# Quantised integers of two BitLinear layers: rounding constant taken off before the transposes, which then move bfloat16 halves

## The chip, the cores and the metric

The kernel runs on one core of a Trainium2 chip. The metric is device time in microseconds. Before the change the median of nine runs is 669.87 us (667.6 to 670.4).

Engines are named as in the profile: PE is TensorE (PEld its weight loads), DVE VectorE, ACT ScalarE, POOL GpSimd and SP SyncE, which issues most of the DMAs.

## The reference, cut to what matters

A small transformer of four layers runs over x of 4 x 256 tokens with 256 features, each layer with an attention and a feed-forward block, all with residuals. The change touches the feed-forward blocks of layers 1 and 2, whose matmuls quantise both operands:

```
def act_quant(x):
    scale = 127.0 / jnp.clip(jnp.max(jnp.abs(x), axis=-1, keepdims=True), EPS)
    return jnp.clip(jnp.round(x * scale), -128.0, 127.0) / scale
def weight_quant(w):
    scale = 1.0 / jnp.clip(jnp.mean(jnp.abs(w)), EPS)
    return jnp.clip(jnp.round(w * scale), -1.0, 1.0) / scale
h = jax.nn.silu(bitlinear(x, w1)) * bitlinear(x, w3)   # layer 1, 704 hidden
return bitlinear(h, w2)
```

Layer 2 does the same with 1024 hidden features and biases. So each row of activations becomes whole numbers from -127 to 127 times one scale per row, and each weight -1, 0 or 1 times one scale. Such numbers are exact in bfloat16.

## The kernel before, in words

The 1024 tokens are eight tiles of 128 rows (two per batch). Before the last feed-forward block, everything is emitted by `layers(nk)`. Its coroutines each describe one piece of work as a sequence of `Op`s: an engine, an assumed duration, the buffers read and written, and new buffers wanted (PSUM banks, and SBUF slots "a2", "a4", "sc"). `Flow.run` (L182) keeps a planned clock per engine. It takes next the operation whose planned start plus `PULL` times its coroutine's due time is smallest, emits the instructions, and moves on. The result is a fixed order on PE, DVE, ACT, POOL and SP. The due times stand in `DUE` by stage (L82, plus `SKEW` per batch) and in `DUE_WEIGHTS` (L83). `func` on an `Op` marks Silu and Exp, for which the trace has ACT load a function table at each switch (1283 ns); the planner charges 1.3 us. The emitted program holds this plan for two cases of the token ids (`nk` 1 and 2); the run takes `nk` = 1.

A tile goes through `token_tile` (L1305): `attention1`, then `ffn1(t)` (L1249). When both tiles of a batch are done, `batch(b)` (L1353) runs the attention of layer 2 and then `ffn2(t)` (L1386) for both, and starts `attention3` of the batch. Layer 3 ends per tile in `tile3`, which routes tokens: POOL scatters eight copies of each row to DRAM by indirect DMA (`hs`, L1677). After the last scatters the experts' stage begins (L1895), which is the same in both kernels.

Both feed-forward functions follow one scheme:

1. `norms` (L850): statistics on DVE, the power -1/2 on POOL (L861), normed rows on DVE (L864).
2. `scales` (L1208): the greatest magnitude of each row (DVE, L1211 to L1213), its products with the weights' means (POOL, L1217), then in place `src * s + ROUND` on DVE (L1221). ROUND is 1.5 * 2^23, so the sum rounds to a whole number, and the tile then holds that number plus ROUND in float32.
3. `turned_ints` (L1224): float32 transposes on PE in chunks of 128 columns, up to four into one PSUM bank (L1235); ACT copies them out to `qT` in bfloat16 and takes ROUND off through the bias (L1239; L1244 for the last chunk of 64 columns in layer 1).
4. Matmuls with the ternary weights, bfloat16 (L1270, L1407), Silu on ACT, the product on DVE (L1277) or POOL (L1422).
5. `scales` and `turned_ints` again over the hidden rows, 704 or 1024 wide, and the last matmul (L1288, L1430).

Of the kernel before, what the change touches and what calls it, by code (L numbers as in the profile page):

```python
# [22 lines left out]
BF16 = mybir.dt.bfloat16  # L23
I32 = mybir.dt.int32
AF = mybir.ActivationFunctionType
ALU = mybir.AluOpType
AX = mybir.AxisListType

P = 128
B, S, D = 4, 256, 256  # L30
# [7 lines left out]
ROUND = 1.5 * 2.0**23  # L38
# [27 lines left out]
def chunks_of(n):  # L66
    return [(i, min(P, n - i)) for i in range(0, n, P)]


PE, DVE, ACT, POOL, SP = "PE", "DVE", "ACT", "POOL", "SP"  # L70
# [8 lines left out]

LATER = 20.0  # L80
PULL, SKEW = 0.00368, 28.0
DUE = dict(x0=0.0, f0=50.0, x1=70.0, f1=100.0, x2=140.0, f2=190.0, q3=140.0, h3=260.0, t3=240.0)  # L82
DUE_WEIGHTS = dict(fp8=80.0, f1=170.0, p2=330.0, f2=160.0, win=250.0, kv=240.0, p3=200.0)  # L83


class Buf:
# [27 lines left out]
class Flow:  # L114
# [21 lines left out]
    def go(self, gen, due=0.0):  # L136
        th = Thread(gen, due)
        self.threads.append(th)
        self.resume(th, None)
        return th  # L140
# [10 lines left out]
    def release(self, *bufs):  # L151

        for b in bufs:
            self.roles[b.role][b.slot] = max(b.used, b.ready or 0.0)
# [76 lines left out]
def model(ctx: ExitStack, tc: tile.TileContext, a: dict, out: bass.AP):  # L231
    nc = tc.nc
# [11 lines left out]
    def scal(n, name):  # L244
        return small.tile([P, n], F32, tag=f"s{n}", name=name)

    def held(pool, shape, name, dtype=F32):
        return pool.tile(shape, dtype, tag=name, name=name)
# [7 lines left out]
    ident = held(const, [P, P], "ident")  # L256
    make_identity(nc, ident)
    identb = held(const, [P, P], "identb", BF16)
# [5 lines left out]
    rnd = held(const, [P, 2], "rnd")  # L264
# [150 lines left out]
    def layers(nk):  # L415
# [4 lines left out]
        def due(b, stage):  # L420
            return DUE[stage] + SKEW * b

# [18 lines left out]
        def bank(shape, name):  # L441
            return ("bank", shape, name)
# [7 lines left out]
        def sc(name):  # L450
            return ("sc", [P, 16], name)
# [165 lines left out]
        def fp8_weights():  # L617
            for o in range(0, 2 * I0, CH):
                for k in range(2):
                    yield from fp8_piece(loads[("w0_gate", "w0_up")[k]], FP8[k][o // CH], o, CH)  # L620
            for o in range(0, 6 * D, CH):
                yield from fp8_piece(loads["w0_down"], FP8[2][o // CH], o, CH)
# [585 lines left out]
        def scales(src, n, k_means):  # L1208

            s = yield Op(DVE, 0.36 + 0.00122 * n, (src,), new=[sc("am")])  # L1210
            nc.vector.tensor_reduce(s[:, 0:1], src.ap, AX.X, ALU.max, apply_absolute_value=True)  # L1211
            nc.vector.tensor_scalar(s[:, 0:1], s[:, 0:1], QEPS, 1.0 / 127.0, ALU.max, ALU.mult)
            nc.vector.reciprocal(s[:, 1:2], s[:, 0:1])  # L1213
            back = Buf()
            yield Op(POOL, 0.18 * len(k_means), (s, *[m for m, _ in k_means]), (back,))
            for k, (_, col) in enumerate(k_means):
                nc.gpsimd.tensor_tensor(  # L1217
                    s[:, 2 + k : 3 + k], s[:, 0:1], means[:, col : col + 1], ALU.mult
                )
            yield Op(DVE, 0.04 + 0.0008 * n, (s,), (src,))  # L1220
            nc.vector.tensor_scalar(src.ap, src.ap, s[:, 1:2], ROUND, ALU.mult, ALU.add)  # L1221
            return s, back

        def turned_ints(src, n, qT):  # L1224

            cs = chunks_of(n)
            groups = [cs[k : k + 4] for k in range(0, len(cs), 4)]
            tps = yield Op(
                PE, 0.122 * len(cs), (src,), new=[bank([P, len(g), P], "tp_q") for g in groups]
            )  # L1230
            if len(groups) == 1:
                tps = [tps]
            for g, tp in zip(groups, tps):
                for k, (o, w) in enumerate(g):
                    nc.tensor.transpose(tp.ap[:w, k, :], src.ap[:, o : o + w], ident)  # L1235
            for i, (g, tp) in enumerate(zip(groups, tps)):
                full = sum(w == P for _, w in g)
                yield Op(ACT, 0.13 + 0.00075 * full * P + (0.25 if full < len(g) else 0), (tp,), (qT,))
                nc.scalar.activation(  # L1239
                    qT[:, 4 * i : 4 * i + full, :], tp.ap[:, :full, :], AF.Identity, bias=rnd[:, 1:2]  # L1240
                )
                if full < len(g):
                    w = g[-1][1]
                    nc.scalar.activation(  # L1244
                        qT[:w, 4 * i + full, :], tp.ap[:w, full, :], AF.Identity, bias=rnd[:w, 1:2]
                    )
            release(*tps)

        def ffn1(t):  # L1249
# [4 lines left out]
            flat = Buf(h.ap[:, 0, :], h.role, h.slot, h.ready)  # L1254
            flat.used = h.used
            s, back = yield from scales(flat, D, [(Q1[0], 0), (Q1[1], 1)])
            yield from turned_ints(flat, D, qT)
            release(flat)
            n = I1 // 2
# [13 lines left out]
            for nh, (pg, pu, g) in enumerate(pre):  # L1273
# [6 lines left out]
                release(pg, pu, g)  # L1280
            release(s)
            s, back = yield from scales(hh, I1, [(Q1[2], 2)])
            yield from turned_ints(hh, I1, qT)
            release(hh)
            cs = chunks_of(I1)
# [100 lines left out]
        def ffn2(t):  # L1386
# [6 lines left out]
            flat = Buf(h.ap[:, 0, :], h.role, h.slot, h.ready)  # L1393
            flat.used = h.used
            s, back = yield from scales(flat, D, [(Q2[0], 3), (Q2[1], 4)])
            yield from turned_ints(flat, D, qT)
            release(flat)
            for nh in range(2):
# [298 lines left out]
        with tc.manual_schedule(engines=ORDERED | {mybir.EngineType.SP}):  # L1697
# [3 lines left out]
            for c in range(NCH):  # L1701
                go(chunk(c), due(2 * c, "x0"))
            w = DUE_WEIGHTS
            go(fp8_weights(), w["fp8"])
# [23 lines left out]
    def ps_tp(shape, name, dtype=F32):  # L1728
        return psum.tile(shape, dtype, tag="tp", name=name, bufs=2)
# [22 lines left out]
    def moe_tile(shape, tag, bufs):  # L1752
        return moe.tile(shape, F32, tag=tag, name=tag, bufs=bufs)
# [43 lines left out]
    with tc.If(rv > 0):  # L1797
        hTs = [moe_tile([P, 2, CH], "hT_left", 2) for _ in range(NCH)]
        for t in range(NT):
            h = layernorm(t, moe, 1)  # L1800
            tp = ps_tp([P, 2, P], "tp_h")
# [3 lines left out]
        with tc.For_i(0, E3, 1) as e:  # L1805
# [4 lines left out]
            for c in range(NCH):  # L1810
                pg, pu = ps_mm([I3, CH], "ps_g3"), ps_mm([I3, CH], "ps_u3")
                for k, ps in enumerate((pg, pu)):
                    for dc in range(2):
                        o = (2 * k + dc) * I3
# [3 lines left out]
                g = moe_tile([I3, CH], "g_left", 1)  # L1818
                nc.scalar.activation(g, pg, AF.Silu)
                nc.vector.tensor_mul(g, pu, g)  # L1820
                for k in range(TPC):
# [3 lines left out]
                    w = scal(1, "w_left")  # L1825
# [245 lines left out]
```

## Time and profile before

| | |
|---|---|
| median of 9 runs | 669.87 us |
| the profiled execution | 669.71 us |
| its span in the trace | 668.0 us |
| its mean granted clock | 0.973 |
| L1235 transposes | 144, from 116.9 to 363 us |
| start of the first and last scatter L1677 | 351.5 and 479.3 us |

Times in the profile count from the span's start. The page gives busy times of engines over the span. The chain of waits follows back from the last instruction, at each step to what released it. A group of instructions has its line, engine, operation, tiles and shapes, then count, busy time, mean duration in ns, and the engine's idle time just before them with what ended it. The last 188 us of the span are the experts' stage.

### The profile page before, as it was taken

To read this page: it belongs to the slowest core of one execution; us is meant where nothing else is said; L and a number is where in the kernel's file an instruction comes from. 1 tells how busy PE (TensorE), PEld (TensorE's weight loads), DVE (VectorE), ACT (ScalarE), POOL (GpSimd) and SP (SyncE) were. 2 spreads that over 40 slices of the span, in tenths; PEclk is the share of its full clock that TensorE was granted. 3 is DMA by queue.
4 is the path that set the end of the run, shared out by engine and by line. 5 is a ranking of instruction groups with operands and counts; after the bars stand their busy time and mean duration, and the time that the engine had idled before them with its cause. 6 is when DMAs were issued, how large, how long until landed. Compare 5 with 4: busy or idle time off the path is not lost.

```text
span 668.0 us, 11511 instructions
## 1 busy us (share of the span) xinstructions
PE 605.8 (91%) x3844; PEld 465.7 (70%) x3844; DVE 462.7 (69%) x1172; ACT 349.0 (52%) x898; POOL 403.3 (60%) x524
## 2 busy tenths in 40 slices
PE   5998699998999999999999899797299999999966
PEld 4764267676787777787778678674188788787754
DVE  5689857875969697599889788887434434434755
ACT  1244248869789874466866696566322222222210
POOL 6998995044454534647447868787746566566550
PEclk9999899999999999999999999899699999999997
DMA  8999999501200130000030111122499887777666
GB/s 292 372 386 235 220 226 239 146 25 29 83 2 1 64 111 2 0 1 1 2 95 33 57 56 47 57 88 85 141 290 357 263 278 252 236 237 215 218 201 233
DMA packets 57059, 98.15 MB, mean 147 GB/s; under 512 B 7121, under 2 KB 39624, under 8 KB 56992
## 3 DMA queue, kind: packets, MB, share of 16 engines
q1 hardware_dynamic: 47072, 78.40, 39.7%
q0 software_dynamic: 7680, 16.84, 7.3%
q10 hardware_dynamic: 2240, 2.10, 0.9%
q8 instruction: 32, 0.52, 0.3%
q14 instruction: 35, 0.29, 0.2%
HBM read 58.42 MB, written 43.07 MB: 152 GB/s over the span
## 4 chain that ended last, share of the span: by engine, by line
PE 53%; DVE 19%; ACT 9%; POOL 8%; issue 6%; DMA 4%; DVEq 0%; POOLq 0%; SPq 0%; ACTq 0%
PE ps_y L1930 7%; PE ps_g L1912 7%; PE ps_q L1463 5%; POOL hs L1677 3%; DVE act L1920 3%; PE ps_u L1912 3%; DMA hs<-hx,slots 2%; PE ps_p L700 2%; PE ps_y L1346 2%; PE ps_u L1078 2%; PE ps_s L1324 2%; PE ps_y L1567 2%; POOL q L1477 1%; PE tp_q L1235 1%; PE ps_p L896 1%
## 5 line engine op out<-in xcount | busy, mean ns | idle before, releaser
L1937 POOL DMA_INDIRECT yd<-yb,hb x84 | 82.5, 982 | 57.9 <-DVE yb L1935 38.6
L1677 POOL DMA_INDIRECT hs<-hx,slots x64 | 67.3, 1052 | 21.9 <-issue 11.3
L861 POOL TENSOR_TENSOR st<-st,mhalf 128x1 f32<-128x1 f32 x56 | 33.0, 593 | 60.5 <-DVE st L857 46.6
L1920 DVE TENSOR_TENSOR act<-ps_u,g 96x384 f32<-96x384 f32 x32 | 17.7, 554 | 65.1 <-ACT g L1918 35.9
L1510 ACT ACTIVATE e<-ps_s,nm 128x128 f32<-128x128 f32 x128 | 45.9, 404 | 15.7 <-DVE nm L1504 15.4
L1477 POOL TENSOR_TENSOR q<-rt 64x512 f32<-64x512 f32 x32 | 44.0, 1376 | 12.1 <-DVE rt L1473 7.4
L1930 PE MATMUL ps_y<-wt,act 96*64 96x256 f32 x336 | 42.4, 388 | 2.7 <-DVE act L1920 1.4
L1912 PE MATMUL ps_g<-hbT,wt 128*96 128x192 f32 x224 | 43.1, 336 | 0.0
L1912 PEld LDWEIGHTS ps_g<-hbT,wt 128*96 128x96 f32 x224 | 34.1, 162 | 10.8 <-issue 10.8
L1912 PE MATMUL ps_u<-hbT,wt 128*96 128x192 f32 x224 | 41.0, 326 | 0.0
L1935 DVE COPY yb<-ps_y 128x256 f32<-128x256 f32 x64 | 27.2, 425 | 19.7 <-PE ps_y L1930 19.5
L1935 ACT COPY yb<-ps_y 128x256 f32<-128x256 f32 x32 | 11.9, 373 | 47.0 <-DVE yb L1935 38.4
L1912 PEld LDWEIGHTS ps_u<-hbT,wt 128*96 128x96 f32 x224 | 36.4, 163 | 0.0
L1422 POOL TENSOR_TENSOR hh<-g,v 128x512 f32<-128x512 f32 x16 | 20.3, 1277 | 25.3 <-ACT g L1420 16.4
L1498 PEld LDWEIGHTS ps_s<-keys,q 128*128 128x128 f32 x256 | 34.5, 196 | 1.3
L1918 ACT ACTIVATE g<-ps_g 96x384 f32<-96x384 f32 x32 | 15.6, 487 | 36.5 <-PE ps_g L1912 36.5
L1498 PE MATMUL ps_s<-keys,q 128*128 128x128 f32 x256 | 34.6, 279 | 0.0
L1930 PEld LDWEIGHTS ps_y<-wt,act 96*64 96x64 f32 x336 | 21.6, 136 | 17.5 <-DVE act L1920 9.4
L1923 ACT COPY hbT<-tp_hb 128x384 f32<-128x384 f32 x31 | 14.8, 479 | 35.0 <-PE tp_hb L1839 35.0
L1239 ACT ACTIVATE qT<-tp_q,rnd 128x512 bf16<-128x512 f32 (+2 forms) x48 | 25.7, 567 | 12.4 <-PE tp_q L1235 12.3
L1510 ACT ACTIVATION_READ_ACCUMULATOR e<-ps_s,nm 128x1 f32 x128 | 30.6, 243 | 0.0
L864 DVE TENSOR_SCALAR h<-x,st 128x256 f32<-128x256 f32 x56 | 27.0, 494 | 5.0 <-POOL st L861 4.8
(345 smaller groups left out, 1728.1 us busy)
## 6 DMA issues: line engine op xcount, KB each, us to landing
hs<-blank_row SPq DMA_DIRECT2D x1, 12336.0 KB, 87.0
hb<-hs SPq DMA_DIRECT2D x28, 385.5 KB, 3.9
wt<-in_w_gu SPq DMA_DIRECT2D x14, 768.0 KB, 8.6
yd<-blank SPq DMA_DIRECT2D x1, 8192.0 KB, 28.9
wt<-yd SPq DMA_DIRECT2D x6, 1024.0 KB, 6.9
wt<-in_w_dn SPq DMA_DIRECT2D x14, 384.0 KB, 8.6
wo<-in_w_o SPq DMA_DIRECT2D x2, 1024.0 KB, 5.7
w<-in_w SPq DMA_DIRECT2D x2, 704.0 KB, 11.2
```

Of the source, the lines that this page charges most:

```text
L861: nc.gpsimd.tensor_tensor(s[:, 8:9], s[:, 7:8], mhalf, ALU.pow)
L864: nc.vector.tensor_scalar(h[:, k, :], x_t(t), ss[k][:, 6:7], ss[k][:, 8:9], ALU.subtract, ALU.mult)
L1463: nc.tensor.matmul(ps.ap[:, k, :], w[:, hp * P : (hp + 1) * P], qc.ap, start=True, stop=True)
L1477: nc.gpsimd.tensor_add(qv(q[i])[r, hps, :], t0[r], t1[r])
L1498: nc.tensor.matmul(s.ap[:, k, :], qv(q[hd % 2])[:, hd // 2, rows], keys3[:, hd % 2, b * S : b * S + nk * P], start=False, stop=k == n - 1,)
L1510: nc.scalar.activation(wide[:, k, :], s.ap[:, k, :], AF.Exp, bias=nm[:, k : k + 1], accum_out=tot[:, k : k + 1],)
L1677: put = nc.gpsimd.indirect_dma_start(out=hs[:, :], out_offset=bass.IndirectOffsetOnAxis(ap=slots[:, t, j : j + 1], axis=0), in_=rows[:, j, ...
L1912: nc.tensor.matmul(ps[:, i], gu[:, (e + i) % GROUP, 2 * k + dc, :], hbT[:, dc, :, i * (P // 2) : (i + 1) * (P // 2)], start=dc == 0, stop= ...
L1920: nc.vector.tensor_mul(act, pu, g)
L1930: nc.tensor.matmul(y[i * (P // 2) : (i + 1) * (P // 2), k], act[:, i, j, :], dn[:, (e + i) % GROUP, :], start=True, stop=True,)
L1935: (nc.scalar.copy if j == 1 else nc.vector.tensor_copy)(yb[:, j, :], y[:, k, :])
L1937: put = nc.gpsimd.indirect_dma_start(out=yd[:, :], out_offset=bass.IndirectOffsetOnAxis(ap=hbs[p][:, j, D : D + 1].bitcast(I32), axis=0), ...
```

## The change

`scales` takes ROUND off again itself. For the normed rows (256 wide, 16 calls) DVE subtracts it; for the hidden rows (704 or 1024 wide, 16 calls) POOL adds -ROUND, a column spread over the row. The tile then holds small whole numbers in float32, whose upper 16 bits are the same number in bfloat16. `turned_ints` transposes these upper halves, read with a stride of two, against the bfloat16 identity into bfloat16 PSUM tiles, and ACT copies them out without a bias. The planner is told half the duration for the transposes, and 10 of its 16 due times are others. Lines from L1250 on are 4 higher in the changed kernel; the transposes are L1243 and the evictions L1247 and L1250.

```diff
--- before.py
+++ after.py
@@ -79,8 +79,8 @@
 
 LATER = 20.0
 PULL, SKEW = 0.00368, 28.0
-DUE = dict(x0=0.0, f0=50.0, x1=70.0, f1=100.0, x2=140.0, f2=190.0, q3=140.0, h3=260.0, t3=240.0)
-DUE_WEIGHTS = dict(fp8=80.0, f1=170.0, p2=330.0, f2=160.0, win=250.0, kv=240.0, p3=200.0)
+DUE = dict(x0=10.0, f0=50.0, x1=70.0, f1=100.0, x2=135.0, f2=185.0, q3=150.0, h3=260.0, t3=220.0)
+DUE_WEIGHTS = dict(fp8=90.0, f1=170.0, p2=430.0, f2=170.0, win=260.0, kv=280.0, p3=200.0)
 
 
 class Buf:
@@ -1219,6 +1219,12 @@
                 )
             yield Op(DVE, 0.04 + 0.0008 * n, (s,), (src,))
             nc.vector.tensor_scalar(src.ap, src.ap, s[:, 1:2], ROUND, ALU.mult, ALU.add)
+            if n == D:
+                yield Op(DVE, 0.04 + 0.0008 * n, (src,), (src,))
+                nc.vector.tensor_scalar(src.ap, src.ap, ROUND, None, ALU.subtract)
+            else:
+                yield Op(POOL, 0.05 + 0.0024 * n, (src,), (src,))
+                nc.gpsimd.tensor_tensor(src.ap, src.ap, rnd[:, 1:2].to_broadcast([P, n]), ALU.add)
             return s, back
 
         def turned_ints(src, n, qT):
@@ -1226,24 +1232,22 @@
             cs = chunks_of(n)
             groups = [cs[k : k + 4] for k in range(0, len(cs), 4)]
             tps = yield Op(
-                PE, 0.122 * len(cs), (src,), new=[bank([P, len(g), P], "tp_q") for g in groups]
-            )
+                PE, 0.06 * len(cs), (src,), new=[("bank", [P, len(g), P], "tp_q", BF16) for g in groups]
+            )
+
+            ints = src.ap.bitcast(BF16).rearrange("p (i two) -> p i two", two=2)[:, :, 1]
             if len(groups) == 1:
                 tps = [tps]
             for g, tp in zip(groups, tps):
                 for k, (o, w) in enumerate(g):
-                    nc.tensor.transpose(tp.ap[:w, k, :], src.ap[:, o : o + w], ident)
+                    nc.tensor.transpose(tp.ap[:w, k, :], ints[:, o : o + w], identb)
             for i, (g, tp) in enumerate(zip(groups, tps)):
                 full = sum(w == P for _, w in g)
                 yield Op(ACT, 0.13 + 0.00075 * full * P + (0.25 if full < len(g) else 0), (tp,), (qT,))
-                nc.scalar.activation(
-                    qT[:, 4 * i : 4 * i + full, :], tp.ap[:, :full, :], AF.Identity, bias=rnd[:, 1:2]
-                )
+                nc.scalar.copy(qT[:, 4 * i : 4 * i + full, :], tp.ap[:, :full, :])
                 if full < len(g):
                     w = g[-1][1]
-                    nc.scalar.activation(
-                        qT[:w, 4 * i + full, :], tp.ap[:w, full, :], AF.Identity, bias=rnd[:w, 1:2]
-                    )
+                    nc.scalar.copy(qT[:w, 4 * i + full, :], tp.ap[:w, full, :])
             release(*tps)
 
         def ffn1(t):
```

## Prediction

> **What bounds the kernel now.** I read the page first (busy times, chain), then the busy times by stage, the chain piece by piece, PE's timeline, the groups by shape, and the answers for single lines.
>
> ```profile
> span 668.0 us, 11511 instructions
> ...
> PE 605.8 (91%) x3844; PEld 465.7 (70%) x3844; DVE 462.7 (69%) x1172; ACT 349.0 (52%) x898; POOL 403.3 (60%) x524
> ...
> PE 53%; DVE 19%; ACT 9%; POOL 8%; issue 6%; DMA 4%; DVEq 0%; POOLq 0%; SPq 0%; ACTq 0%
> ```
>
> TensorE is the busiest engine, and over half of the chain that ended last runs through it. By stage:
>
> ```profile
> 100.00:160.00 60.00, 57.72 (x493) 43.15 (x492) 44.70 (x121) 48.44 (x145) 19.75 (x31) 0.97 0.46 115
> 160.00:360.00 200.00, 196.43 (x1248) 155.12 (x1248) 162.81 (x404) 147.28 (x347) 107.15 (x138) 1.00 0.10 33
> 360.00:480.00 120.00, 97.15 (x590) 74.65 (x588) 96.02 (x279) 76.75 (x256) 93.55 (x149) 0.95 0.20 69
> ```
>
> Columns after the length: PE, PEld, DVE, ACT, POOL. The changed steps lie between 115 and 370 us, nearly all in the second row, where PE is busy 98% and DVE 81%, ACT 74%, POOL 54%. A busy matmul overlaps the next, so I also counted each matmul only until the next one's start, and no longer than its columns stream: about 181 of those 200 us. PE is the bound there, with some 19 us of true gaps. After 480 us come the experts; the change leaves them alone.
>
> **PE: 144 transposes, each half as long.** Eight tiles turn 2 + 6 chunks (ffn1) and 2 + 8 (ffn2): 8 × 18 = 144. What one costs on a full queue is read from the chain, whose pieces run from start to start:
>
> ```profile
> 243.33 0.66 PE tp_q L1235 x6
> 243.99 0.87 PE ps_y L1430 x8
> ...
> 272.92 0.43 PE ps_g L1407 x2
> ```
>
> A float32 transpose takes 0.66/6 = 0.110 us. The bfloat16 matmuls take 0.109 us for 256 columns (L1430) and 0.215 us for 512 (L1407): time follows columns. PE's timeline has one shorter kind, 64 columns with a full weight load before each:
>
> ```profile
> 456.38 0.34 PE L1599 MATMUL ps_pos<-sel,onesb 128*128 128x64 bf16 x6
> ```
>
> The last one alone lasts 0.19 us, so five steps take 0.15 us, 0.03 each. A 128-column bfloat16 transpose lies between, at 0.055 us: 144 × 0.055 = 7.9 us of PE's queue. Loads of strided halves exist already (the fp8 weights at L1078) and take 104 and 98 ns beside 98 for plain ones, so the stride is free. Of the 144, 76 stand on the chain, 9.2 us together; halved, 4.2 us leave the chain for certain. The rest also stand in the queue that is 90% full. I take −6.0 us, between 4.2 and 7.9; nothing at all is the end of a rival below.
>
> [...]
>
> **DVE: 16 more passes over the normed rows.** The constant is taken off by a second scalar operation of the same shape as L1221.
>
> ```profile
> L1221 DVE TENSOR_SCALAR h<-h,am 128x256 f32<-128x256 f32 x16 | 5.7, 361 | 0.1
> L1422 POOL TENSOR_TENSOR hh<-g,v 128x512 f32<-128x512 f32 x16 | 20.3, 1277 | 25.3 <-ACT g L1420 16.4 <-DVE w L1614 5.0 <-DVE v L1413 3.7
> L1239 ACT ACTIVATE qT<-tp_q,rnd 128x512 bf16<-128x512 f32 x24 | 15.8, 687 | 10.7 <-PE tp_q L1235 10.6
> L1275 ACT ACT_TABLE_LOAD x3 | 3.8, 1283 | 0.1
> ```
>
> 16 × 0.345 us (its undisturbed time) = 5.5 us. From 115 to 370 us DVE is busy 205.4 us, of which 36.0 lie on the chain, 17.5%: +1.0 us. DVE has 50 us of gaps there, so less is possible; all 5.5 is the other end.
>
> **POOL: 16 adds over the hidden rows.** The nearest row is L1422, two-input and of the same tiles: 1277 ns for 512 elements, 2.5 ns each. 704 elements give 1.76 us, 1024 give 2.55: 8 × 4.31 = 34.5 us. What hides it: POOL is busy 126.4 of the 255 us, so 129 are free. Each add is a new link: transposes that waited for DVE's L1221 now wait for POOL, and PE's whole queue stands behind them. On POOL the norms' powers (L861), the scale products (L1217) and the query sums (L1477) queue behind the add; DVE's L864 and with it the next tile's transposes wait for the powers. In the changed program's order all 16 adds stand ahead of the first scatter, so the scatters, POOL's load after 350 us, are not interleaved with them. L1422, same engine, same tiles, never appears on the chain in 16 times; I take 0. At POOL's mean share of the chain (26.0 of 126.4 us, 20.6%) it would be +7.1 us. If the cover goes, a tile's path is longer by 0.35 + 1.76 us in ffn1 and 0.35 + 2.55 in ffn2, 5.0 in all.
>
> A side effect on DVE: the same operation is slower beside POOL work.
>
> ```profile
> L864 DVE TENSOR_SCALAR h<-x,st x56: 395/408/1473, 10.4 to 395.3; 128x256 f32<-128x256 f32 x56
> L1527 DVE TENSOR_TENSOR e<-e,nm x32: 691/692/1905, 299.8 to 457.1; 128x512 f32<-128x512 f32 x32
> ```
>
> Beyond their medians these two lose 56 × (494 − 408) and 32 × (807 − 692) ns = 8.5 us in the whole run, beside about 215 us of POOL arithmetic. For 34.5 us more that is 1.4 us of DVE, at 17.5% +0.3 us.
>
> **ACT.** The 56 evictions become plain copies from bfloat16. No row has that input; the nearest copies (L1155, float32, same size) take 602 ns beside 687. From −0.085 × 24 = −2.0 us to +2.0; I take 0. The built program's order, instruction by instruction, holds something the diff does not tell: 19 function table loads before the experts instead of 15, since Silu and Exp are interleaved differently. 4 × 1.283 = 5.1 us of ACT; its share of the chain is 37.8 of 188.5 us, 20%: +1.0 us, from 0 to 5.1.
>
> **The order.** The due times move by up to 100 us (p2), and every engine's order changes with them. SP issues the same transfers in the same sequence; DMA costs stay. Summing row durations along PE's order, the last batch's first query product (L1463) stands behind 338 us of PE work, 345 before, so PE's saving is not spent in front of it. Whether the new order has more or fewer waits no row shows: PE's named waits from 100 to 380 us come to some 8 us, so −8 to +8; I take 0.
>
> **Sum.** The profiled execution took 669.7 us (span 668.0), practically the median, 669.9. −6.0 + 1.0 + 0 + 0.3 + 0 + 1.0 = −3.7: **666.0 us**.
>
> **Rivals.** *POOL takes PE's place* (slower). Place: the wait of the tp_q transposes, from 120 to 365 us. Price: chain terms alone: −4.2 + 1.0 + 0.3 + 1.0 + 7.1 = +5.2, 674.9 us. It decides once over half of the adds' 34.5 us × 20.6% shows; for it speaks that the adds double the POOL work of a hidden layer, against it POOL's 129 idle us and L1422. *The full PE gain* (better): 7.9 us, with 2.0 from the evictions, and DVE's, ACT's and contention's terms hidden: 659.8 us. For it: PE 90% full. *The transposes do not get cheaper*: the load of a float32 transpose takes 141 ns and a bfloat16 one 98, so if loads set the pace at 0.11 us, only the costs stay: 669.7 + 2.3 = 672.0 us. Against it: the 0.03 us row.
>
> **How the numbers follow.** Forecast 50%, POOL rival 25%, full gain 13%, no cheaper transposes 7%, 5% for an order that misses all of these. A measurement of this kernel can tell about 0.2% from no change, 1.3 us. Of the forecast's 50, 7 fall within that and 43 are faster; the full gain adds 13, the odd orders 2: 58% faster. Of the POOL rival's 25, 4 lie within, of the 7 one, making 12 with the forecast's; 30% are slower. The low end takes the full gain and 1.8 of the 8 us of waits, 658; the high end reaches the POOL rival, 675.
>
> **What would show it.** Right: tp_q start to start near 0.055 us; PE busy from 160 to 360 us without POOL as releaser of tp_q; the experts' first rows land some 4 us earlier. Wrong: waits "PE tp_q <- POOL hh" of several us, table loads on the chain beyond two, tp_q at 0.08 or more, or gaps on PE that come from the order and lie away from the changed lines.

## The result and the profile after

The changed kernel takes 675.50 us (median of 10 runs, 673.12 to 676.55); before, run beside it, takes 669.88 us (31 runs). The ratio is 1.0077, interval 1.0063 to 1.0091. I had forecast 666.0, between 658 and 675. The profiled execution took 676.24 us, its span 674.5.

The page of the changed kernel:

```profile
span 674.5 us, 11551 instructions
...
PE 607.6 (90%) x3844; PEld 460.8 (68%) x3844; DVE 477.6 (71%) x1188; ACT 349.5 (52%) x902; POOL 428.3 (63%) x540
...
PE 46%; DVE 26%; POOL 9%; issue 7%; ACT 6%; DMA 4%; POOLq 0%; DVEq 0%; SPq 0%; ACTq 0%
```

POOL and DVE got the work that was added, 25 and 15 us. The last line is the news: PE's share of the chain went from 53% to 46%, DVE's from 19% to 26%. By stage (columns after the length: PE, PEld, DVE, ACT, POOL):

```profile
100.00:160.00 60.00, 58.30 (x511) 43.03 (x509) 48.97 (x134) 51.15 (x154) 26.06 (x37) 1.00 0.50 130
160.00:360.00 200.00, 189.54 (x1203) 145.08 (x1204) 168.70 (x397) 139.43 (x322) 125.42 (x146) 0.97 0.08 27
360.00:480.00 120.00, 103.38 (x621) 79.81 (x619) 101.01 (x290) 82.18 (x278) 90.31 (x144) 0.94 0.19 66
```

In the second row PE is busy for 189.5 us where it had 196.4, but the stage is not shorter: the first scatter starts at 358.2 us, 351.5 before. The transposes themselves became as narrow as the change makes them. One piece of the changed kernel's chain (start, length, work), then its groups of new and changed operations by shape:

```profile
253.05 0.45 PE tp_q L1243 x8
```

```profile
L1227 POOL TENSOR_TENSOR hh<-hh,rnd 128x1024 f32<-128x1024 f32 x8 | 16.4, 2051 | 2.1 <-DVE hh L1221 1.8
L1227 POOL TENSOR_TENSOR hh<-hh,rnd 128x704 f32<-128x704 f32 x8 | 11.1, 1389 | 1.5 <-DVE hh L1221 1.2
L1224 DVE TENSOR_SCALAR h<-h 128x256 f32<-128x256 f32 x16 | 7.7, 490 | 0.2
L1247 ACT COPY qT<-tp_q 128x512 bf16<-128x512 bf16 x24 | 13.9, 595 | 1.5 <-PE tp_q L1243 1.4
```

A transpose takes 0.45/8 = 0.056 us from start to start, 0.110 before. The adds take 16.4 + 11.1 = 27.5 us of POOL, the evictions 595 ns where they took 687. But the subtraction's mean of 490 ns is far above its median of 294. DVE's and POOL's timelines show why, of the changed kernel, each line with start, length and what ran, and in brackets the idle time before it with what ended that:

```profile
319.38 0.30 DVE L1224 TENSOR_SCALAR h<-h 128x256 f32<-128x256 f32 x1
...
324.46 1.98 DVE L1224 TENSOR_SCALAR h<-h 128x256 f32<-128x256 f32 x1
```

```profile
320.96 3.04 POOL L1481 TENSOR_TENSOR q<-rt 64x512 f32<-64x512 f32 x2 [1.23 <-DVE rt L1477]
324.07 2.22 POOL L1227 TENSOR_TENSOR hh<-hh,rnd 128x1024 f32<-128x1024 f32 x1
```

The same subtraction takes 0.30 us without an add beside it and 1.98 us when it starts behind an add on POOL; it ends at 326.44, 0.15 us after the add. So I read it as DVE standing until the add is over, not as DVE running slower beside it. L864 and L1221 stand in the same way (L864 for 0.56 to 2.12 us where its median is 0.41; L1221 on the normed rows: 606 ns in the mean, 361 before). Eight of the 16 adds meet a DVE scalar operation over 256 columns (L864, L1221, L1224 or L1666). All eight of these end 0.149 to 0.152 us after their add, while they last 0.51 to 2.12 us, and together they last 8.4 us more than by their lines' medians. Reductions (L1211, 1.21 us over 1024 columns), statistics (L855, 0.42 us) and operations that read PSUM (L1417, 0.74 us) have the same lengths beside the adds as without. It works the other way too: an add over 1024 columns takes 1.89 us at its shortest, and 2.10 to 2.27 us in the four cases where L1221 or L1531 was already at work on DVE as it starts.

In one of the eight, L864 at 302.99 us, the DVE record begins 0.07 us ahead of the add's (303.06 us), and DVE stands all the same, for 2.12 us; that add keeps its 1.89 us. What makes DVE stand no run shows, only when it goes on.

Adding up, per form, what DVE's instructions from 115 to 372 us take beyond their lower quartile gives some 9 us in the before kernel and some 19 in the changed one.

### The profile page after: what moved, and what is told of

It reads as the page before. It is cut to its first block, busy times and chain, and to the rows that moved or that the text cites. A ratio compares the mean times of both kernels' runs of the same rounds, so it can differ in the third digit from the quotient of the medians.

```text
span 674.5 us, 11551 instructions
## 1 busy us (share of the span) xinstructions
PE 607.6 (90%) x3844; PEld 460.8 (68%) x3844; DVE 477.6 (71%) x1188; ACT 349.5 (52%) x902; POOL 428.3 (63%) x540
## 4 chain that ended last, share of the span: by engine, by line
PE 46%; DVE 26%; POOL 9%; issue 7%; ACT 6%; DMA 4%; POOLq 0%; DVEq 0%; SPq 0%; ACTq 0%
PE ps_y L1934 7%; PE ps_g L1916 7%; POOL hs L1681 3%; PE ps_g L1078 3%; DVE act L1924 3%; PE ps_u L1078 2%; PE ps_u L1916 2%; PE ps_y L1350 2%; PE ps_y L1127 2%; PE ps_q L1467 2%; DVE e L1531 2%; PE ps_s L1328 2%; DVE h L864 1%; PE tp_e L1151 1%; DVE am L1211 1%
## 5 line engine op out<-in xcount | busy, mean ns | idle before, releaser
L1481 POOL TENSOR_TENSOR q<-rt 64x512 f32<-64x512 f32 x32 | 42.3, 1320 | 11.9 <-DVE rt L1477 4.6
L1502 PEld LDWEIGHTS ps_s<-keys,q 128*128 128x128 f32 x256 | 34.5, 196 | 2.8 <-issue 1.1
L1934 PEld LDWEIGHTS ps_y<-wt,act 96*64 96x64 f32 x336 | 21.6, 136 | 17.5 <-DVE act L1924 9.4
L864 DVE TENSOR_SCALAR h<-x,st 128x256 f32<-128x256 f32 x56 | 29.4, 534 | 5.2 <-POOL st L861 4.8
L1571 PE MATMUL ps_y<-bo,u 128*128 128x256 f32 x128 | 29.6, 383 | 1.3 <-ACT u L1556 0.7
L1143 ACT ACTIVATE e<-ps_s,nb 128x256 f32<-128x256 f32 x64 | 29.9, 489 | 1.5 <-DVE nb L1140 1.5
L1467 PE MATMUL ps_q<-qc,wq 96*128 96x256 f32 x128 | 30.5, 381 | 0.0
```

Source lines behind the costliest of these rows:

```text
L864: nc.vector.tensor_scalar(h[:, k, :], x_t(t), ss[k][:, 6:7], ss[k][:, 8:9], ALU.subtract, ALU.mult)
L1467: nc.tensor.matmul(ps.ap[:, k, :], w[:, hp * P : (hp + 1) * P], qc.ap, start=True, stop=True)
L1481: nc.gpsimd.tensor_add(qv(q[i])[r, hps, :], t0[r], t1[r])
L1502: nc.tensor.matmul(s.ap[:, k, :], qv(q[hd % 2])[:, hd // 2, rows], keys3[:, hd % 2, b * S : b * S + nk * P], start=False, stop=k == n - 1,)
L1934: nc.tensor.matmul(y[i * (P // 2) : (i + 1) * (P // 2), k], act[:, i, j, :], dn[:, (e + i) % GROUP, :], start=True, stop=True,)
```

## The experiments

**How they are compared.** Start-up, which holds no changed step, differs between executions (the first matmul `ps_y` of L1127 starts between 90.4 and 94.1 us). And on two of the chips used, where before takes 679 and 685 us instead of 670, every kernel run there has one or two waits of 3.6 to 9.9 us after 380 us whose release the trace does not name, and the other kernels have none of this kind. So beside the ratio I give the stretch **S**, from the first L1127 matmul to the first scatter: it holds every changed step. Repeated executions of one kernel differ in S by 0 to 1.7 us. What follows S, to the end of the last scatter, takes 131.4 us in the before kernel, 130.5 in the changed one. (The last scatter of before starts at 481.9 us, not at the 479.3 of the table above.)

| run | transposes | subtraction | adds | S, us | ratio to before, interval |
|---|---|---|---|---|---|
| before (two executions) | float32 | - | - | 260.6, 259.8 | 1 |
| e7 | float32 | - | - | 260.8 | 1.0023, 1.0009 to 1.0037 |
| e11 | bfloat16 | - | - | 258.6 | 0.9994, 0.9967 to 1.0022 |
| e3, e3b | bfloat16 | DVE | - | 258.2, 258.2 | 0.9996, 0.9970 to 1.0022; 0.9987, 0.9961 to 1.0013 |
| e5 | bfloat16 | - | POOL | 262.7 | 1.0015, 0.9994 to 1.0036 |
| after, a2 | bfloat16 | DVE | POOL | 266.2, 267.9 | 1.0077, 1.0063 to 1.0091; 1.0105, 1.0087 to 1.0124 |
| e4, e4b | float32 | DVE | POOL | 266.9, 268.4 | 1.0256, 1.0225 to 1.0286; 1.0125, 1.0060 to 1.0189 |
| e8 | bfloat16 | DVE | DVE | 266.4 | 1.0068, 1.0045 to 1.0092 |
| e9 | bfloat16 | DVE | POOL, into a spare tile | 265.0 | 1.0055, 1.0035 to 1.0076 |
| e10 | bfloat16 | DVE | ACT | 265.6 | 1.0075, 1.0046 to 1.0104 |
| e12 | bfloat16 | DVE | POOL, PE kept busy | 266.8 | 1.0103, 1.0058 to 1.0148 |

All from e7 down run in the order of the changed kernel: in their traces the order of the operations on each engine is the same. Three more, in the order of before: e6 (all passes, adds on POOL) 280.5, e13 (adds on DVE) 268.8, e14 (normed rows alone) 259.3. Most rows rest on one traced execution, so differences of S under 2 us say little.

**First question: code or order?** Two kernels swap the due times. e1 is the old code with the new ones, e2 the new code with the old ones (cut to one of the two lines, as e1 changes it; e2 is the reverse):

```diff
-DUE = dict(x0=0.0, f0=50.0, x1=70.0, f1=100.0, x2=140.0, f2=190.0, q3=140.0, h3=260.0, t3=240.0)
+DUE = dict(x0=10.0, f0=50.0, x1=70.0, f1=100.0, x2=135.0, f2=185.0, q3=150.0, h3=260.0, t3=220.0)
```

> The code of before (float32 transposes, the constant taken off in the eviction) with the ten new due times. Theory POOL (the 16 GpSimd adds, 27.5 us of POOL's queue, cost what the change costs): the due times alone do little, 668 to 672 us. Theory ORDER (the replanned order costs it, not the code): 674 to 677 us. In between, 672 to 674, both have a share.

> The changed code with the due times of before. POOL: the adds still stand in the queue, 674 to 679 us. ORDER: the loss is gone and TensorE's saving shows, 664 to 668 us.

Measured: 703.78 us, ratio 1.0363 (1.0332 to 1.0394), and 701.53 us, 1.0315 (1.0280 to 1.0350). Both lie over 20 us above the highest that either theory allowed. Only 9.5 us of that are the chip's, where before takes 679.34 us: each code is slow with the other's due times. S is 266.0 and 267.6; from the first scatter to the end of the last another 158.7 and 152.4 us pass, against 142.3 in e3 on the same chip. The planner makes from each pair of code and due times an order that is neither that of before nor that of the changed kernel. So a new plan is a change of its own, as large as anything studied here, and code and order have to be parted with the order held fixed.

**Code and order apart.** The old code in exactly the changed kernel's order (e7: the added `Op`s are planned but nothing is emitted for them), the changed code in exactly the order of before (e6: planned with the costs of before, the new instructions put in behind L1221), and both kernels again (b2, a2), in one set (the diff is cut to what differs from the changed kernel):

```diff
 # e7, against after: planned, not emitted; turned_ints as in before
                 yield Op(DVE, 0.04 + 0.0008 * n, (src,), (src,))
-                nc.vector.tensor_scalar(src.ap, src.ap, ROUND, None, ALU.subtract)
                 yield Op(POOL, 0.05 + 0.0024 * n, (src,), (src,))
-                nc.gpsimd.tensor_tensor(src.ap, src.ap, rnd[:, 1:2].to_broadcast([P, n]), ALU.add)
 # e6, against after: emitted, not planned; due times of before
-                yield Op(DVE, 0.04 + 0.0008 * n, (src,), (src,))
                 nc.vector.tensor_scalar(src.ap, src.ap, ROUND, None, ALU.subtract)
-                yield Op(POOL, 0.05 + 0.0024 * n, (src,), (src,))
                 nc.gpsimd.tensor_tensor(src.ap, src.ap, rnd[:, 1:2].to_broadcast([P, n]), ALU.add)
-                PE, 0.06 * len(cs), (src,), ...
+                PE, 0.122 * len(cs), (src,), ...
```

> The kernel before, unchanged, for a trace beside the other three of this set: every theory expects a ratio of 0.998 to 1.002 to itself.

> The changed kernel, unchanged, as the fourth corner of this set: a ratio to before of 1.006 to 1.009 as measured at first. If it is above 1.012, the ratio depends on more than the kernels, and the other ratios of the set are to be read against this one.

> The changed code (subtraction on DVE, adds on POOL, bfloat16 transposes, copies on ACT) in the order of before: the planner sees the due times and the costs of before, and the 16 + 16 new instructions are put in directly behind L1221, so that PE, ACT and SP run the very sequence of before. Theory POOL (the adds cost more than TensorE saves, in any order): 1.004 to 1.010. Theory ORDER (the code saves what my sum said, the new order loses it): 0.990 to 0.997.

> The code of before (float32 transposes, the constant taken off in the eviction, no added passes) in the very order of the changed kernel: its due times and planned costs are kept, the new instructions are planned but not emitted. POOL: 0.997 to 1.003, since no add is there. ORDER: 1.010 to 1.020; the sum of the two runs before (adds worth 5.4 us, transposes worth 12) gives 1.016.

Measured: b2 1.0008 (0.9997 to 1.0018), a2 1.0105 (1.0087 to 1.0124, a little above its range), e7 1.0023 (1.0009 to 1.0037), e6 1.0333 (1.0313 to 1.0354). ORDER falls: the new order costs the old code 671.41 - 669.76 = 1.6 us, the changed code costs 4.8 us more in it, and 22.5 in the order of before. POOL got e7 right and e6's sign, with a loss over three times what it expected. In e6 the wait is where I had told readers to look. PE's waits of e6 (its add is L1225, its transposes L1241) from 115 to 372 us (us in total, times, longest):

```profile
PE tp_q L1241 <- POOL hh L1225: 12.7, 9, 3.6
```

In the changed kernel this line does not exist (its weight loads wait for an add once, for 0.5 us); its longest PE waits in that stretch are others:

```profile
PE ps_ab L642 <- DVE ab L637: 2.4, 1, 2.4
PE tp_h L876 <- DVE h L864: 1.9, 2, 1.4
```

The planner knew of the adds there and put other matmuls ahead of the transposes. So the absence of a wait for POOL does not say that the adds are free. The chain shows where the time goes. The page of e7, the old code in the same order, has:

```profile
PE 61%; DVE 17%; ACT 7%; POOL 6%; issue 5%; DMA 3%; DVEq 0%; POOLq 0%; SPq 0%; ACTq 0%
```

I added the chain's pieces from 115 to 372 us: in e7 196.5 us of PE and 20.8 of DVE, in the changed kernel 112.7 of PE and 83.5 of DVE (119.4 and 82.1 in a2). With the passes in, the bound has moved from PE to DVE for a good part of the way. One place of both chains, e7 first, then the changed kernel:

```profile
302.80 0.97 POOL st L861
303.80 0.41 DVE h L864
304.21 0.67 DVE g L1417
304.93 0.38 PE ps_s L1495
```

```profile
301.99 0.97 POOL st L861
302.97 0.02 issue
302.99 2.12 DVE h L864
305.11 0.66 DVE g L1417
305.76 0.66 DVE v L1417
306.42 0.10 DVE nm L1530
...
319.61 1.27 DVE rt L1477 x2
320.88 0.66 DVE hh L1221
321.54 1.27 DVE h L1221
322.81 0.10 DVE nm L1530
322.91 0.02 issue
322.93 1.61 DVE e L1531
324.54 1.90 DVE h L1224
```

In e7 the chain leaves PE for 4 us, 300.8 to 304.9. In the changed kernel it stays on DVE from 294 us on (with short pieces of POOL), and L864, L1221, L1531 and L1224 stand in it at 2.3 to 6.7 times their undisturbed lengths (0.41, 0.35, 0.69 and 0.29 us). L864 and L1224 stand behind adds (at 303.06 and 324.07 us); L1221 and L1531 run beside POOL's query sums L1481, which both kernels have, and end 0.15 and 0.55 us after them; so the adds account for a part of this piece only. From the second to the third batch's query product (L1467) e7 takes 40.4 us and e3, without the adds, the same; the changed kernel takes 44.2, and 45.9 in a2.

**The parts one by one, in the changed kernel's order.** e3 leaves out the adds, e5 the subtractions, e11 both; e4 goes back to float32 transposes with both passes in; e3b and e4b repeat e3 and e4 (cut to the lines that matter):

```diff
 # e3, e11
-                nc.gpsimd.tensor_tensor(src.ap, src.ap, rnd[:, 1:2].to_broadcast([P, n]), ALU.add)
 # e5, e11
-                nc.vector.tensor_scalar(src.ap, src.ap, ROUND, None, ALU.subtract)
 # e3, e5, e11 (and e9), so that numbers that keep the constant go nowhere
-            nc.vector.scalar_tensor_tensor(x_t(t), y.ap, s[:, 2:3], x_t(t), ALU.mult, ALU.add)
+            nc.vector.scalar_tensor_tensor(x_t(t), y.ap, 0.0, x_t(t), ALU.mult, ALU.add)
 # e4 (its PSUM tiles are float32 again)
-                    nc.tensor.transpose(tp.ap[:w, k, :], ints[:, o : o + w], identb)
+                    nc.tensor.transpose(tp.ap[:w, k, :], src.ap[:, o : o + w], ident)
```

> The changed kernel in its own order, with the 16 GpSimd adds of the hidden rows left out (so the hidden integers keep the constant, and the feed-forward results of layers 1 and 2 are added to x with the factor 0). POOL: at least the whole loss comes back, 664 to 669 us; the first clock drop after 200 us, 217 to 224 us in the changed kernel, is gone or lies elsewhere. ORDER: the order is the same, so the time stays at 673 to 676 us.

> The changed kernel in its own order, with the constant taken off first as there, but the integers transposed as float32 again: only TensorE's saving is taken back (144 x 0.055 = 7.9 us of its queue) and the evictions read float32. If TensorE's queue still sets the pace (my prediction's step): 4.2 to 7.9 us more, 679.5 to 683.5 us. If the waits for POOL and DVE have taken its place: within 1.5 us of the changed kernel, 674 to 677 us.

> The changed kernel in its own order, with only the 16 DVE subtractions of the normed rows left out (their integers keep the constant, and the feed-forward results of layers 1 and 2 are added to x with the factor 0). Theory LOCK (DVE has become the bound, because it stands still while POOL adds: 19.4 us of excess between 115 and 372 us against 9.0 without the adds): DVE's 7.7 us less shows, 0.999 to 1.004 of before. Theory LINK (the adds cost as a longer path of each hidden tile to its transposes): my term of 1 us, 1.007 to 1.010.

> The changed kernel in its own order with bfloat16 transposes, but neither the 16 subtractions nor the 16 adds are emitted (the integers keep the constant, and the feed-forward results of layers 1 and 2 are added to x with the factor 0): TensorE's saving alone, beside the old code in this order (671.4 us, 1.0023 of before). If TensorE is the bound once the passes are away (its share of the chain in the old code in this order is 197 of 258 us): 7.9 x 197/258 = 6.0 us less, 0.991 to 0.996 of before. If the saving is worth nothing even then: 1.000 to 1.004.

> As e4: both passes in, float32 transposes, the order of the changed kernel; set beside the three other corners of the same chip. If the bound has moved from TensorE to the passes, the transposes' width is worth nothing here: 1.007 to 1.012 of before, like the changed kernel. If TensorE still sets the pace: 1.014 to 1.022.

> As e3: the adds left out (the hidden integers keep the constant, and the feed-forward results of layers 1 and 2 are added to x with the factor 0), subtractions and bfloat16 transposes in. From e3's trace, ahead of the changed kernel by 8 us at the third batch's query product: 0.995 to 0.999 of before. If the adds matter only together with that chip: 1.005 to 1.010.

Measured as in the table. e3, e3b and e5 fit the theory that blames the adds (e3's ratio of 0.9996 is the whole loss given back; its half clock at 217 us is 3.4 us long, not gone), e5 that of DVE's standstill; e4 lies above both of its ranges, e4b between its two, with an interval that reaches into both. e3, e5 and e11 compute with other numbers than the changed kernel; e9 below keeps the same constant as e3 and most of the loss, so in e3 the numbers are not what takes it away. The **adds** cost 266.2 - 258.2 = 8.0 us of S (9.7 with a2) beside the subtractions, and 262.7 - 258.6 = 4.1 without them. The **subtractions** cost nothing alone (258.6 to 258.2), and 3.5 to 5.2 us beside the adds. This is no sum of parts; that the two passes meet on DVE, which the adds hold up, would explain it, and no run shows it by itself. The **narrow transposes**, with their shorter evictions, save 260.8 - 258.6 = 2.2 us with the passes away, little more than two executions of one kernel differ (1.7 us). e11 lies between its two ranges: the gain is neither 6.0 us nor nothing. With the passes in, e4 and e4b (266.9, 268.4) lie 0.6 us above after and a2 in the mean, less than two executions of one kernel differ: the width of the transposes is worth nothing there that I can tell. The ratios of e4 (1.0256) and e4b (1.0125) do not agree with each other and are larger than S allows; both ran on the chips with the longer waits after 380 us, so I do not read the end-to-end price of float32 transposes from them.

**Does it matter who runs the adds?** e8 puts them on DVE, e10 on ACT, and e9 leaves them on POOL but out of every path (cut: the spare tile, and the factor 0 shown above):

```diff
-                nc.gpsimd.tensor_tensor(src.ap, src.ap, rnd[:, 1:2].to_broadcast([P, n]), ALU.add)
+                nc.vector.tensor_scalar(src.ap, src.ap, ROUND, None, ALU.subtract)                      # e8
+                nc.scalar.activation(src.ap, src.ap, AF.Identity, bias=rnd[:, 1:2])                      # e10
+                for o in range(0, n, n // 4):                                                            # e9
+                    nc.gpsimd.tensor_tensor(
+                        spare[:, : n // 4], src[:, o : o + n // 4], rnd[:, 1:2].to_broadcast([P, n // 4]), ALU.add
+                    )
```

> The changed kernel in its own order, the constant of the hidden rows taken off by DVE in place of POOL: from L1221 and L1224 of the trace (285 ns for 256, 578 for 704) about 0.52 us for 704 and 0.69 for 1024, 9.7 us more on DVE, while 27.5 us of POOL and some 8.5 us of standstill go. LOCK and LINK both expect a gain on the changed kernel, to 0.998 to 1.004 of before. If DVE's queue is what sets the pace, whoever fills it, it stays at 1.007 to 1.011.

> The changed kernel in its own order, where the 16 adds run on POOL at their place (in four pieces each, for want of room) but write to a spare tile that nobody reads, so no transpose waits for them (the hidden integers keep the constant, and the feed-forward results of layers 1 and 2 are added to x with the factor 0). LOCK: POOL's time and DVE's standstill are all there, 1.005 to 1.011 of before. LINK: the path is short again, 0.996 to 1.002, as without the adds.

> The changed kernel in its own order, the constant of the hidden rows taken off by ACT (Identity with a bias) in place of POOL: the path of a tile keeps a link of about 0.7 and 1.0 us, ACT gets about 13 us, POOL's 27.5 us and DVE's standstill go. LOCK: 0.997 to 1.003. LINK: half of the loss stays, 1.003 to 1.008.

Measured: 1.0068, 1.0055 and 1.0075; S 266.4, 265.0 and 265.6, all within 3 us of the changed kernel and 7 to 8 above e3. e9 lies in LOCK's range and e10 in LINK's; e8 misses both and lies just under the third, of DVE's queue. LOCK and LINK both fall as single causes: e8 and e10 have no adds to stand behind, e9 has no link, and each keeps most of the loss. For DVE the sum agrees: in S it is busy for 221.4 us in the changed kernel and 221.1 in e8, the 10.4 us of its own passes in place of the 8.4 of standing. The chain of e8 from 115 to 372 us has 114.9 us of DVE and 92.1 of PE; e10's has 53.4 of ACT (16.6 in the changed kernel), and in e9's the adds that nobody waits for lie on the chain with 18.9 us. So in each version the engine that got the pass gained on the chain. e9 is a blunt test, though: its 64 pieces kept POOL busy for 166.2 us of S, 9.5 more than the adds did, and DVE stands only some 3 us beside them.

**The clock.** In the changed kernel the granted clock is at half from 217.0 to 223.8 us, right behind PE's wait at L642. e12 fills that wait (cut: the wider bank that the filling needs):

```diff
+            for _ in range(21 if col == 5 else 0):
+                nc.tensor.matmul(ps.ap, ones, ident, start=True, stop=True)
             nc.tensor.matmul(ps.ap, ones, ab[:, :n_parts], start=True, stop=True)
```

> The changed kernel with 21 matmuls of no use (2.3 us of TensorE, into the bank of the sum that follows) directly ahead of the sum at L642 for which TensorE waits 2.4 us at 213 us; the granted clock is at half there from 215.0 to 221.8 us. Theory CLOCK (the gap is what brings the half clock, and that multiplies the loss): the window at 215 us is gone or half as long, 1.5 to 3.5 us less than the changed kernel, 1.004 to 1.008 of before. Theory PLAIN WAIT (the clock falls for another reason, or other work is late anyway): 1.007 to 1.012.

Measured: 1.0103 (1.0058 to 1.0148), S 266.8. PE's timeline of e12:

```profile
216.75 4.96 PE L643 MATMUL ps_ab<-ident,ones 128*128 128x128 f32 x42
221.54 0.28 PE L646 MATMUL ps_ab<-ab,ones 128*128 128x2 f32 x2
```

The filling took 5.0 us and not 2.3: its 21 float32 matmuls stand in the trace as 42. Counted from the first L1127 matmul the sum came 2.4 us later than in the changed kernel. The half clock is gone there, and from the sum to the first query product 49.2 us pass instead of 51.2. So the clock had cost about 2 us at this place, by one execution of each kernel, and no more than the filling did. The total lies in the range of PLAIN WAIT. In all, e12 has 3.4 us of half clock within S, like e7 and e3, and after has 10.2; but e12's S is that of the changed kernel. The clock is at most a small part of the loss, not its cause.

**Why so much worse in the old order?** e13 is e6 with the adds on DVE; e14 keeps only the subtractions and the 32 transposes of the normed rows, the hidden rows as in before (cut: e14's narrow transposes and copies of these rows):

```diff
 # e13, against e6
-                nc.gpsimd.tensor_tensor(src.ap, src.ap, rnd[:, 1:2].to_broadcast([P, n]), ALU.add)
+                nc.vector.tensor_scalar(src.ap, src.ap, ROUND, None, ALU.subtract)
 # e14, against before
+            if n == D:
+                nc.vector.tensor_scalar(src.ap, src.ap, ROUND, None, ALU.subtract)
```

> The changed code in the order of before (as e6), but the hidden rows' constant is taken off by DVE in place of POOL, directly behind L1221: the link to the transposes shrinks from 1.39 and 2.05 us to about 0.52 and 0.69, POOL runs as in before, DVE gets 9.7 us more. If e6's 22 us are the adds' link and POOL's queue: 1.000 to 1.008 of before. If any pass that the order was not planned with costs this much: 1.020 to 1.035.

> The order of before, and only the normed rows changed: DVE takes the constant off the 16 rows of 256 (about 4.6 us of DVE), their 32 transposes run as bfloat16 (1.8 us of TensorE) and are copied; the hidden rows stay as before, with no add. If the adds are what costs in that order: 0.997 to 1.004 of before. If the subtractions carry a third or more of e6's loss: 1.010 to 1.020.

Measured: e13 682.56 us, 1.0175 (1.0154 to 1.0196); e14 670.42 us, 1.0005 (0.9985 to 1.0025). Without the hidden rows' pass the loss is gone, in this order as in the other: the normed rows' part alone is free, and gains nothing. Here the changed code costs 22 us with the pass on POOL and 12 with it on DVE, which is between the two ranges that I had set. PE waits for it there directly; PE's waits of e13 from 115 to 372 us, its pass on DVE being L1225:

```profile
PE tp_q L1241 <- DVE hh L1225: 6.2, 6, 2.1
```

No kernel of the study beats before beyond its interval, so there was no better version to run: the best, e3b, leaves out work and stands at 0.9987.

## Why the prediction was wrong

The step that failed first is "POOL: 16 adds over the hidden rows ... I take 0". I sized the adds well enough (34.5 us estimated, 27.5 measured), but took them to be hidden by POOL's 129 idle us and by L1422's absence from the chain. They cost 8.0 to 9.7 us of S beside the subtractions, 4.1 without. My own alternative in that step, POOL's mean share of the chain, gave +7.1. Idle time of an engine covers a pass only if nothing waits for the pass and the other engines go on meanwhile; here a tile waits, and DVE stands behind eight of the 16 adds. That L1422 was not on the chain said that the order had room around L1422, not that it had room for another pass behind it.

The second failure is "−6.0 us, between 4.2 and 7.9" for PE. The duration was right, 0.056 us measured for 0.055 taken. But a PE that is 98% busy is not a PE that alone sets the pace. With no pass added, the 7.9 us of its queue bring 2.2 (e7 to e11, shorter evictions included), less than the 4.2 that I called certain from the chain; with the passes in, 0.6 or nothing. The chain of one execution counts what was last; it does not say how closely the next engine follows.

- **DVE, +1.0**: alone nothing, beside the adds 3.5 to 5.2. The passes were 7.7 us long instead of 5.5, because they too stood behind POOL.
- **Contention, +0.3**: mis-sized at the root. I spread past losses evenly over POOL's work, 1.4 us for 34.5; the adds brought 8.4 (5.9 beside the 1024 wide, 2.5 beside the 704 wide), and DVE's chain share had meanwhile gone from 36.0 to 83.5 us of the same stretch. (1.4 us at 17.5% is also 0.2, not 0.3.)
- **Evictions, 0**: 0.09 us shorter each (512 wide), on an engine that did not bind; no run isolates it.
- **Table loads, +1.0, and order, 0**: e7 holds both, +1.6 us. These steps held. The changed kernel's trace has 20 loads ahead of 480 us and that of before 17, three more and not four; two stand on the chain in both.

Of the rivals, POOL in PE's place named the right side and nearly the size (674.9 for 675.5), the size partly by luck, since the errors of its terms offset each other in part: PE's −4.2 came as −2.2 at most, DVE's +1.3 as nothing by itself, the adds' +7.1 as 8.0 to 9.7. Its place was wrong: not the transposes' wait, which the planner had filled, but, by the chain, DVE's and POOL's queues. "The transposes do not get cheaper" falls by the 0.056 us. What is shown is that the pass over the hidden rows makes the loss: without it the loss is gone, in both orders. What stays open is how the adds' cost divides between the path of a tile, POOL's queue and DVE's standing; e8, e9 and e10 each take one or two away, put other work in their place, and each gets back 3 us or less. A version with the standing alone was not tried.

## What to carry to other kernels

Before paying for a saving on the busiest engine with a pass elsewhere, sum the busy times of every engine over the same stretch: here the next one, DVE, stood at 81%, the saving was small and the pass was not free. Price a long POOL operation not only with POOL's idle time, but also with the DVE operations that the trace shows standing behind such work (here scalar operations over 256 columns, for up to 1.7 us each). Where an order is planned, part code from order by emitting each code in the other's order before judging either.

## What the runs showed of the hardware

- A POOL add of a one-column operand takes 1.36 us for 704 and 1.89 us for 1024 elements at its shortest, a difference of 1.7 ns for each further element. The means of 1389 and 2051 ns hold adds that began while a DVE operation was at work (1.40 and 1.57 us; 2.10 to 2.27 us).
- DVE's scalar operations over 256 columns in SBUF that meet such an add end 0.15 us after it, in all eight cases of the changed kernel; reductions beside it keep their lengths (L1211 over 1024 columns: 1.21 us with and without).
- Spans of half clock last 3.4, 10.2 and 13.7 us in the trace of before and 3.4, 6.8 and 20.5 us in that of the changed kernel (without the last of each, which the end of the trace cuts off): all close to multiples of 3.4 us. What sets that length no run shows.
- A wait of 2.3 to 2.4 us at L642 was followed by 3.4 us of half clock in e7 and e3 and by 6.8 in the changed kernel, so the wait alone does not fix the loss.
- Chips differ: before takes 670 us in four of the six sets, and 679 and 685 on the chips of the other two. The kernels run there have waits that no others have, such as 5.5 us of DVE's before L1507 in e3; the trace does not name what ends them, and why these chips differ stays open.
